# Mixer: convolutions from shifted rows laid out through HBM, output sums in PSUM, pieces spread over slots, light slots filled with zero-weight matmuls

## The chip, the cores and the metric

The kernel runs on one core of one Trainium2 chip, in one launch. A core has five engines with instruction streams of their own: TensorE (PE), VectorE (DVE), ScalarE (ACT), GpSimd (POOL) and SyncE (SP), which here issues the DMAs. They meet only at semaphores. The metric is the time of one execution on the device in microseconds. "PEld" in the profile is PE's loading of weights, which overlaps its matmuls. Everything is in 32-bit floats.

## The reference

Input `x` is 8 sequences of 256 tokens with 128 features. Six blocks are added to it in turn: a network of six small attentions (twice, with a 16-head attention between), a mixture of 8 experts with the best 2 per token, a mixer, and the same experts again.

```python
x = x + 0.5 * ffn(layernorm(x)); x = x + attention(layernorm(x)); x = x + 0.5 * ffn(layernorm(x))
x = x + 0.5 * experts(layernorm(x))
x = x + mixer(layernorm(x))
x = x + 0.5 * experts(layernorm(x))

# mixer, hidden [b, l, 128]; DI = 256 channels, DS = 16 states, DR = 64, K = 4 taps
xz = einsum('bld,ed->bel', hidden, in_proj_w)              # 512 rows: x and z
def branch(xz, ...):                                       # once forward, once on xz[:, :, ::-1]
    x, z = split(xz, 2, axis=1)
    x = silu(causal depthwise convolution(x, conv_w [256, 1, 4]) + bias)
    dt, B, C = x_proj(x)                                   # 64 + 16 + 16 rows
    delta = softplus(dt_proj(dt) + dt_bias)
    h = exp(delta * A) * h + delta * B * x                 # a scan over the tokens, per channel and state
    y = sum over states of h * C + D * x
    return y * silu(z)
# third branch: a 2-D FFT of x, a width-5 convolution over frequencies with 512 x 512 weights, silu,
# an inverse FFT, times max(silu(z)), absolute value, and a layer norm of that: out_f
out = einsum('bdl,od->blo', out_forward + out_backward[:, :, ::-1] + out_f, out_proj_w)
```

The causal convolution of a channel `c` is `sum over k of w[c, k] * x[c, l + k - 3]`: each channel stands alone. The backward branch is the same with the taps counted from the other side.

## The kernel before

The 2048 tokens are 4 chunks of 512 (`NCH` = 4), each of two sequences and of four tiles of 128 tokens. The two networks and the attention come first; the change doesn't touch them. The rest is one function, `experts_and_mixer`. It holds the first experts, the mixer and the second experts, and it writes them as a list of slots.

The mixer's 256 channels are two tiles `t` of 128 partitions, its directions are `r` = 0 and 1. Channel and state are spread over partitions in units: a chunk has 32 units (`t`, `r`, a channel group `i` and a half `jp`), 128 in all. A unit `n` takes these steps:

- `spread`: matmuls with 0/1 weights copy rows of `dl` (delta) and `du` (delta times x) from 32 rows to 128 partitions (line 1197), 32 rows deep. Two go into `pU`, a pair of PSUM banks with two buffers; two go into single banks ("p" banks, three in all), from which ACT makes `dA` = exp(A * delta) (line 1199; four buffers).
- `feed`: DVE multiplies `pU` with `B` (line 1206).
- `scan`: DVE runs the scan (line 1217, two buffers `h`); POOL multiplies `h` with `C` into `hc` (line 1219).
- `sums`: on every second slot, eight matmuls with 0/1 weights add two units' `hc` into the bank of `y`, 32 columns each (line 1236).

Slot `i` holds in this order: scan of unit `i`, feed of unit `i + 1`, the pieces that `at(i, ...)` lists, on odd slots the sums of units `i - 3` and `i - 2`, the pieces listed with `last=True`, then the spread of unit `i + 2` with some units' dA. The order is written out by hand for PE, DVE, ACT and POOL (a manual schedule: each engine takes its instructions in exactly this order). SP has its own queue, and takes its DMAs in the order in which they were written. Slots before 0 are a prologue, where the first experts' 16 tiles are interleaved (`first.step`), and slots after 127 an epilogue with the second experts.

The pieces of a chunk, by their names and lines:

- `normalize` makes the layer norm. `features` transposes it into `xT`, which has three zero columns at either end (line 1059). `gate` makes `sz` from `xT` (line 1069).
- `convolve(ch, t, r)` makes the projection and the convolution in one: four matmuls, one per tap, of 128 x 128 weights and 512 columns, on `xT` at four shifts, summed in a PSUM bank (line 1082). Their weights `inK` are the projection times the tap, multiplied on DVE in `taps` (line 872), where `inK` arrives as a table of 1 MB. ACT copies the result into `u`.
- `ranks`, `rows`, `steps`, `softplus`, `delta` make `B`, `C`, `dl` and `du`. `steps` is two matmuls, 64 rows deep (line 1133). `delta` has a product on POOL (line 1155) and two DMAs that exchange halves of `du` (lines 1158 and 1159).
- `skip` adds `D * u` into the bank of `y` (line 1226); `weigh` multiplies `y` with `sz`.
- The FFT branch: `frequencies`, `pairs` (POOL), `mix` (ten matmuls each, line 1280), `mirror`, `halves` (POOL, line 1306), `over_channels`, `folds` (POOL), `over_tokens` (lines 1312 and 1313 for both), `squares`, `magnitude`, `moments`, `whiten`. It runs up to 32 slots behind the scans of its chunk. Around two slots in a chunk (`bursts`) ACT changes its table for SiLU; no dA is made there, and more of it some slots later.
- `join` adds the FFT branch to `sz` on POOL (line 1416), `output` projects with eight matmuls of 128 columns and copies to `o`, `add` adds `o` to `x` on POOL (line 1437).

In the prologue, chunk 0's convolutions stand in slots -15 to -12. The weights of the FFT branch are folded there too: `fetch` loads 1 MB tables `s_fft` one after the other, `fold_pairs` adds and subtracts them on POOL and DVE (line 921 is a small DMA of each), and `transform` and `conv_weights` multiply them (lines 883 and 934).

Of the kernel before, what the change touches and what calls it, by code (L numbers as in the profile page):

```python
# [17 lines left out]
P = 128  # L18
# [797 lines left out]

def experts_and_mixer(nc, tc, ident, nhalf, x, cols, ins, w, given, store):
# [19 lines left out]
    with ExitStack() as ctx:  # L837
        pool = ctx.enter_context(tc.tile_pool(name="mamba", bufs=1))
        ps = psum(ctx, tc)

# [5 lines left out]
        xT = pool.tile([P, 2, S + 6], F32, name="xT")  # L846
        nc.gpsimd.memset(xT[:, :, 0:3], 0.0)
        nc.gpsimd.memset(xT[:, :, S + 3 :], 0.0)
        xTm = xT[:, :, 3 : S + 3]
# [4 lines left out]

        tiny = pool.tile([P, 1], F32, name="tiny")
# [5 lines left out]
        def at(slot, f, *a, last=False):  # L861
            (after if last else before).setdefault(slot, []).append(lambda: f(*a))
# [5 lines left out]

        def taps(r, t):

            to = w["inK"][:, r, t]
            nc.vector.tensor_tensor(to, to, bcast(w["inT"][:, t * P : (t + 1) * P], K), ALU.mult)
# [172 lines left out]
        def normalize(ch, part):  # L1045
            got = gots[ch]
            h = part % 2
            xh = x[ch][:, 2 * h : 2 * h + 2, :]
            if part < 2:
                got["stats", h] = ln_scales(nc, pool, nhalf, xh, 1e-5)  # L1050
                return
            if h == 0:
                got["xn"] = given["xT"].rearrange("p (t d) -> p t d", t=NT)
            ln_scaled(nc, xh, got["xn"][:, 2 * h : 2 * h + 2, :], got["stats", h])

        def features(ch):
# [5 lines left out]
            nc.scalar.copy(xTm, pt)  # L1062

        def gate(ch, t):
            got = gots[ch]
            if t == 0:
# [3 lines left out]
                pz, w["inT"][:, DI + t * P : DI + (t + 1) * P], xTm, start=True, stop=True  # L1070
            )
            nc.scalar.copy(got["sz"][:, t, :], pz.rearrange("p b l -> p (b l)"))

        def convolve(ch, t, r):
# [5 lines left out]
            for k in range(K):  # L1080
                o = k if r == 0 else 2 * (K - 1) - k
                nc.tensor.matmul(  # L1082
                    pu, w["inK"][:, r, t, k, :], xT[:, :, o : o + S], start=(k == 0), stop=(k == K - 1)
                )
# [20 lines left out]
        def ranks(ch, r):  # L1105

            got = gots[ch]
            if r == 0:
                got["low"] = pool.tile([LOW, 2, CT], F32, tag="low", name="low")
            px = bank([P, CT])[0:LOW, :]  # L1110
            for t in range(2):
                nc.tensor.matmul(  # L1112
                    px, w["xproj"][:, r, t, :], got["u", t][:, r, :], start=(t == 0), stop=(t == 1)
                )
            nc.scalar.copy(got["low"][:, r, :], px)

        def rows(ch, r, k):
# [4 lines left out]
            n = DR + DS * k  # L1122
# [3 lines left out]
        def steps(ch, t, r):  # L1126

            got = gots[ch]
            if r == 0:
                got["dl", t] = pool.tile([P, 2, CT], F32, tag=f"dl{t}", name=f"dl{t}")  # L1130
# [750 lines left out]
```

## Time and profile before

| | us |
|---|---|
| median of three runs (1972.27 to 1981.3) | 1974.96 |
| profiled execution, its own time | 1971.64 |
| its span in the profile | 1969.9 |
| first scan starts | 1352.8 |
| last scan starts | 1896.9 |

Busy in the whole span: PE 1860.1 us (94%), PEld 1143.3, DVE 1503.3 (76%), ACT 1019.3 (52%), POOL 1074.3 (55%). The mean granted clock of TensorE is 0.98 of full speed. These are shares over stages with different limits; the stage that matters here is that of the 128 scans. There a group's row tells, in this order, line, engine, operation, the tile written and those read, shapes, and the count; then the busy time in us, the mean of one in ns, the idle time of the engine just ahead of these instructions, and what ended most of it. A line of waits names the engine and line that waited, the one that ended the wait, the total in us, how often, and the longest. Matmuls overlap each other, so the mean of one is longer than its distance to the next: where a matmul's cost is meant, the distance from one group's start to the next instruction's is taken.

### The profile page before, as it was taken

How to read it: one execution, taken by the hardware profiler on the slowest of the kernel's cores; microseconds unless marked ns; L12 is line 12 of the kernel's file. 1: busy time of each engine (PE TensorE's matmuls, PEld its weight loads, DVE VectorE, ACT ScalarE, POOL GpSimd, SP SyncE). 2: the span in 40 equal slices, each digit the busy share in tenths (PEclk: the TensorE clock that was granted, in tenths of full speed). 3: DMA queues.
4: the chain of work that ended last, by engine and by line, in shares of the span. 5: the costliest groups of instructions: out<-in, count | busy, mean ns of one | idle time of the engine just before them, and what ended most of it. 6: DMA issues, size and time to landing. Idle time of an engine off the chain costs nothing. (4 is left out here: it accounts for less than half of the span.)

```text
span 1969.9 us, 45628 instructions
## 1 busy us (share of the span) xinstructions
PE 1860.1 (94%) x17792; PEld 1143.3 (58%) x17792; DVE 1503.3 (76%) x2573; ACT 1019.3 (52%) x1911; POOL 1074.3 (55%) x1399
## 2 busy tenths in 40 slices
PE   6999999998999999899999999799989999989888
PEld 5777777764565666577777776453344344345345
DVE  5777777787878777577777777647997887997874
ACT  2666666662333222166666666445555654654544
POOL 4333333357666655433333334644878787787864
PEclk9999999998999999899999999999999999999899
DMA  4000000000000000000000000321000010000000
GB/s 151 3 3 3 3 3 3 3 3 1 2 2 2 2 2 2 1 3 3 3 3 4 3 3 3 113 72 26 12 22 22 0 30 15 12 21 12 0 1 22
DMA packets 21242, 29.27 MB, mean 15 GB/s; under 512 B 12506, under 2 KB 13914, under 8 KB 20260
## 3 DMA queue, kind: packets, MB, share of 16 engines
q1 hardware_dynamic: 20740, 26.15, 4.5%
q8 instruction: 142, 2.33, 0.5%
q14 instruction: 72, 0.59, 0.1%
q10 hardware_dynamic: 288, 0.20, 0.0%
HBM read 16.10 MB, written 1.05 MB: 9 GB/s over the span
## 5 line engine op out<-in xcount | busy, mean ns | idle before, releaser
L350 DVE TENSOR_REDUCE negmax<-sc 128x2 f32<-128x512 f32 x768 | 475.0, 677 | 126.7 <-PE sc L342 126.4
L355 ACT ACTIVATE ex<-sc 128x512 f32<-128x512 f32 x768 | 398.0, 603 | 231.9 <-PE sc L342 231.9
L342 PE MATMUL sc<-qk,qk 32*128 32x256 f32 x6144 | 423.1, 397 | 8.0 <-DVE tp L393 2.7
L342 PEld LDWEIGHTS sc<-qk,qk 32*128 32x128 f32 x6144 | 309.8, 187 | 109.7 <-issue 65.5
L1219 POOL TENSOR_TENSOR hc<-h,C 128x1024 f32<-128x1024 f32 x128 | 301.3, 2357 | 112.0 <-DVE h L1217 106.9
L298 POOL TENSOR_SCALAR qk<-qkraw,head_rows,w_bqk 128x256 f32<-128x256 f32 x384 | 207.8, 555 | 203.8 <-ACT qkraw L294 197.8
L1217 DVE TENSOR_TENSOR_SCAN h<-dA,pU 128x1024 f32<-128x1024 f32 x128 | 292.1, 2282 | 13.4 <-POOL hc L1219 0.9
L406 POOL TENSOR_TENSOR cn<-tp,rec 128x256 f32<-128x256 f32 x96 | 59.5, 620 | 287.1 <-DVE rec L404 287.1
L1199 ACT ACTIVATE dA<-p,cols 128x512 f32<-128x512 f32 x256 | 162.1, 684 | 102.8 <-PE p L1197 100.6
L1206 DVE TENSOR_TENSOR pU<-pU,B 128x1024 f32<-128x1024 f32 x128 | 155.7, 1216 | 59.0 <-PE p L1197 51.8
L385 PE MATMUL pc<-ex,va 128*32 128x256 f32 x3072 | 185.7, 382 | 0.3 <-ACT ex L355 0.3
L639 ACT ACTIVATE ex<-sc 128x512 f32<-128x512 f32 x128 | 66.1, 603 | 204.5 <-PE sc L624 204.5
L1197 PE MATMUL pU<-du,s_sel 32*128 32x512 f32 x512 | 146.4, 645 | 19.5 <-DVE h L1217 14.0
L1197 PE MATMUL p<-dl,s_sel 32*128 32x512 f32 x512 | 154.2, 635 | 4.3 <-ACT dA L1199 4.2
L624 PE MATMUL sc<-rot,rot 32*128 32x256 f32 x2048 | 135.2, 388 | 0.3 <-POOL rot L607 0.3
L385 PEld LDWEIGHTS pc<-ex,va 128*32 128x32 f32 x3072 | 90.0, 109 | 78.1 <-ACT ex L355 28.0
L642 POOL TENSOR_TENSOR both<-ex 128x512 f32<-128x512 f32 x64 | 80.0, 1271 | 71.7 <-ACT ex L639 71.7
L624 PEld LDWEIGHTS sc<-rot,rot 32*128 32x128 f32 x2048 | 97.9, 184 | 35.1 <-issue 22.6
L634 DVE TENSOR_REDUCE anegmax<-sc 128x2 f32<-128x512 f32 x128 | 79.4, 683 | 22.1 <-PE sc L624 22.1
L1197 PEld LDWEIGHTS pU<-du,s_sel 32*128 32x128 f32 x512 | 40.3, 185 | 89.6 <-issue 65.2
L393 DVE STREAM_TRANSPOSE tp<-pc 128x512 f32<-128x512 f32 x96 | 68.6, 715 | 28.0 <-PE pc L385 28.0
L1010 POOL TENSOR_TENSOR sg_hT<-sg_hT,hid 128x512 f32<-128x512 f32 x32 | 40.5, 1267 | 65.9 <-ACT sg_hT L1009 65.9
(293 smaller groups left out, 3098.7 us busy)
## 6 DMA issues: line engine op xcount, KB each, us to landing
qk<-turned SPq DMA_DIRECT2D x768, 1.0 KB
s_fft<-s_fft SPq DMA_DIRECT2D x5, 1024.0 KB
du<-ab SPq DMA_DIRECT2D x16, 256.0 KB
B<-low SPq DMA_DIRECT2D x64, 32.0 KB
C<-low SPq DMA_DIRECT2D x64, 32.0 KB
x<-x SPq DMA_DIRECT2D x4, 256.0 KB
s_inK<-s_inK SPq DMA_DIRECT2D x1, 1024.0 KB
out<-x SPq DMA_DIRECT2D x4, 256.0 KB
```

What stands on the lines that cost most here:

```text
L298: nc.gpsimd.tensor_scalar(t[:, g, :], raw[:, i, :], w["mask"][:, g : g + 1], w["bqk"][:, c, i, g : g + 1], ALU.mult, ALU.add,)
L342: nc.tensor.matmul(sc[:, t, :], lhs[:, t * P : (t + 1) * P], rhs, start=True, stop=True)
L350: nc.vector.tensor_reduce(sh[:, :, 4 * g + j], sc, AX.X, ALU.max, negate=True)
L355: nc.scalar.activation(ex, sc, AF.Exp, scale=FD**-0.5)
L385: nc.tensor.matmul(st["pc"][32 * j : 32 * j + 32, g, :], st[2][:, kt, 2 * j + g, :], st["ex", g, j][:, kt, :], start=(kt == 0), stop=(kt = ...
L624: nc.tensor.matmul(sc[j][:, t, :], lhs[r, part, t * P : (t + 1) * P] if part < 2 else sel[r, :], rhs[r, part, :] if part < 2 else st["nm"] ...
L642: nc.gpsimd.tensor_tensor(both, ex[:, :, 0], ex[:, :, 1], ALU.add)
L1197: nc.tensor.matmul(dst, w["sel"][rs, i, :], src[rs, :], start=True, stop=True)
L1199: nc.scalar.activation(dA, pA, AF.Exp, scale=rate)
L1206: nc.vector.tensor_tensor(dB, dB, bcast(gots[ch]["B", r], 2), ALU.mult)
L1217: nc.vector.tensor_tensor_scan(hf, af, bf, 0.0, ALU.mult, ALU.add)
L1219: nc.gpsimd.tensor_tensor(hc, h, bcast(gots[ch]["C", r], 2), ALU.mult)
```

## The change

- **Convolution.** A new piece `inputs(ch, t)` does the projection alone (one matmul), copies it to SBUF, writes its rows to HBM in four DMAs, and reads them back in four more, into `shifted`: there partition `32 k + c` holds row `c` of each group of 32 channels, shifted by `k` tokens, so that the four taps of a channel lie on four partitions. `convolve` becomes four matmuls, one for each group of 32 channels, with a 128 x 32 matrix of taps (`s_taps`, 256 KB), each into 32 partitions of the PSUM bank. `taps` and the 1 MB table `s_inK` go; `xT` loses its zero columns, and shares a buffer with `mag`, the copied rows share one with `sq`.
- **Steps.** `low` of direction 1 puts `dt` on partitions 64 to 127, so that the two directions' matmuls of `steps` use different rows of the array; they stand together, each into a bank of its own.
- **Output.** `join` and `add` go. `output(ch, h)` does a half of the tiles: PSUM sums the gated term, the FFT term and `x` itself (times the identity), 10 matmuls of 128 columns, and ACT copies the sum into `x`.
- **Spreads.** The order of a spread's matmuls goes by the rows that they use; where two units' dA are made in a slot, it is listed in `wide`, and the bursts move so that the dA keep their parity.
- **Slots.** Pieces move: `inputs` at slots 2 and 10 of the count that starts a chunk ahead of its scans, `convolve` at 6, 8, 13 and 14 (before at 2, 6, 8, 10), `steps`, `delta`, `mix`, `halves` and what follows them some slots later, `pairs` in four single steps. Chunk 0 has `inputs` last in slots -15 and -13, `convolve` two at a time in -13 and -11.
- **Filler.** `keep_busy`: in slots 0 to 127, where PE's work by a table (`work`) is under `BUSY` = 1.9 us, as many matmuls with zero weights, 128 x 128 on 256 columns, as fill it. They add zero to the bank of `y`, or go to an empty one.

```diff
-        def taps(r, t):
-
-            to = w["inK"][:, r, t]
-            nc.vector.tensor_tensor(to, to, bcast(w["inT"][:, t * P : (t + 1) * P], K), ALU.mult)
...
+        def inputs(ch, t):
+
+            px = bank([P, 2, S])
+            xT = gots[ch]["xT"]
+            nc.tensor.matmul(px, w["inT"][:, t * P : (t + 1) * P], xT, start=True, stop=True)
+            xs = pool.tile([P, 2, S], F32, tag="sq", name="xs", bufs=2)
+            nc.scalar.copy(xs, px)
+            there = hbm.tile([32, 4, 2, S], F32, tag="xs", name="xs_rows")
+            for g in range(4):
+                nc.sync.dma_start(out=there[:, g], in_=xs[32 * g : 32 * g + 32])
+            for k in range(K):
+                nc.sync.dma_start(
+                    out=shifted[32 * k : 32 * k + 32, :, :, K - 1 - k : K - 1 - k + S],
+                    in_=there,
+                )
...
-            for k in range(K):
-                o = k if r == 0 else 2 * (K - 1) - k
+            for g in range(4):
                 nc.tensor.matmul(
-                    pu, w["inK"][:, r, t, k, :], xT[:, :, o : o + S], start=(k == 0), stop=(k == K - 1)
+                    pu[32 * g : 32 * g + 32],
+                    w["taps"][:, r, t, g, :],
+                    shifted[:, g, :, 3 * r : 3 * r + S],
+                    start=True,
+                    stop=True,
                 )
...
+            pds = [bank([P, CT]) for _ in range(2)]
+            for r, pd in enumerate(pds):
+                rs = slice(DR * r, DR * r + DR)
+                nc.tensor.matmul(
+                    pd,
+                    w["dtT"][rs, t * P : (t + 1) * P],
+                    got["low"][rs, r, :],
+                    start=True,
+                    stop=True,
+                )
...
+        def keep_busy(k):
+
+            y = live.get("y")
+            to = bank([P, S]) if k and y is None else y
+            for _ in range(k):
+                nc.tensor.matmul(
+                    to[:, 0:S], zeros, w["G"][:, 0, 0, :], start=y is None, stop=y is None
+                )
...
-        def join(ch):
-            got = gots[ch]
-            nc.gpsimd.tensor_tensor(
-                got["sz"], got["sz"], got["mag"].rearrange("p t b l -> p t (b l)"), ALU.add
-            )
...
+            terms = (got["sz"], got["mag"].rearrange("p t b l -> p t (b l)"))
+            po = bank([P, 2, D])
+            for i in range(2):
+                t = 2 * h + i
+                for v, y in enumerate(terms):
+                    for d in range(2):
+                        nc.tensor.matmul(
+                            po[:, i, :],
+                            y[:, d, t * P : (t + 1) * P],
+                            w["outT"][:, d, :],
+                            start=(v == d == 0),
+                            stop=False,
+                        )
+                nc.tensor.matmul(po[:, i, :], ident, x[ch][:, t, :], start=False, stop=True)
+            nc.scalar.copy(x[ch][:, 2 * h : 2 * h + 2, :], po)
-        def add(ch):
-            nc.gpsimd.tensor_tensor(x[ch], x[ch], gots[ch]["o"], ALU.add)
...
-        for i in range(4):
-            at(-15 + i, convolve, 0, 1 - i // 2, i % 2)
-        at(-11, gate, 0, 0)
-        at(-10, gate, 0, 1)
+        for t in (1, 0):
+            at(-13 - 2 * t, inputs, 0, t, last=True)
+            at(-14, gate, 0, 1 - t)
+            at(-11 - 2 * t, convolve, 0, t, 0)
+            at(-11 - 2 * t, convolve, 0, t, 1)
...
-                at(o + 2, convolve, ch, 1, 0)
-                at(o + 6, convolve, ch, 1, 1)
-                at(o + 8, convolve, ch, 0, 0)
-                at(o + 10, convolve, ch, 0, 1)
...
+                at(o + 2, inputs, ch, 1)
+                at(o + 10, inputs, ch, 0)
+                at(o + 3, gate, ch, 0, last=True)
+                at(o + 4, gate, ch, 1, last=True)
+                at(o + 6, convolve, ch, 1, 0)
+                at(o + 8, convolve, ch, 1, 1)
+                at(o + 13, convolve, ch, 0, 0)
+                at(o + 14, convolve, ch, 0, 1)
...
-            mixes = (4, 6, 8, 9, 11, 12, 14, 15) if final else (11, 13, 18, 20, 22, 23, 24, 25)
+            mixes = (4, 6, 7, 8, 12, 13, 14, 15) if final else (8, 12, 18, 20, 22, 24, 26, 28)
...
-            k = o + (17 if final else 27)
+            k = o + (17 if final else 30)
             bursts.add(k)
             if not final:
-                bursts.add(o + 12)
+                bursts.add(o + 15)
+                wide |= {o + 22, o + 23, o + 34, o + 35}
...
-                    more = next(((0, 0, 1, 2, 1, 1, 2)[i - b] for b in bursts if 0 <= i - b < 7), 1)
+                    more = 0 if i in bursts or i - 1 in bursts else 2 if i in wide else 1
+                busy = 0.43 * (1 + more) + 0.85 * (i % 2)
+                busy += sum(work.get(f, 0) for f, _ in before.get(i, []) + after.get(i, []))
+                if 0 <= i < N:
+                    keep_busy(max(0, math.ceil((BUSY - busy) / 0.43)))
```

## The prediction

> **What bounds the kernel now.** I read the page's slices first, then cut the span by stage (windows), then asked in the stage that changes who waits for whom (the waits and the groups), and last followed one stretch piece by piece (the chain). The change touches only the mixer: its prologue before the first scan at 1352.8 us, its 128 scan slots, and its epilogue after 1896.9 us. The windows below are the prologue, the four chunks of 32 scans, and the epilogue; columns are window, length, busy time of each engine (instructions), clock of PE, DMA share, GB/s.
>
> ```profile
> 1245.00:1352.80 107.80, 95.23 (x408) 55.73 (x411) 54.27 (x154) 57.22 (x96) 49.50 (x67) 0.98 0.29 96
> 1352.80:1481.60 128.80, 120.09 (x540) 46.98 (x540) 119.37 (x82) 72.69 (x114) 95.22 (x67) 0.97 0.06 14
> 1481.60:1619.00 137.40, 129.84 (x618) 57.00 (x616) 119.27 (x87) 79.39 (x125) 111.03 (x86) 1.00 0.07 16
> 1619.00:1756.20 137.20, 129.77 (x617) 57.00 (x616) 118.08 (x78) 79.37 (x125) 108.11 (x78) 1.00 0.07 16
> 1756.20:1896.90 140.70, 125.44 (x609) 62.40 (x609) 116.34 (x102) 65.11 (x107) 114.74 (x85) 0.94 0.03 7
> 1896.90:1969.90 73.00, 59.99 (x322) 39.68 (x320) 38.46 (x126) 36.50 (x63) 34.64 (x39) 0.97 0.04 15
> ```
>
> In the middle chunks DVE works 118 to 119 of 137 us, PE shows 130, POOL 108 to 111. A slot needs the scan (2.28) and the feed (1.21) on DVE, 3.54 us start to start when nothing is late; 32 of them are 113, and DVE's other work (weigh, delta, largest, statistics) makes about 123 us a chunk. So about 14 us of a middle chunk are lost. To whom, in the scan stage (total us, times, longest):
>
> ```profile
> POOL hc L1219 <- DVE h L1217: 105.7, 66, 6.7
> DVE pU L1206 <- PE p L1197: 51.8, 48, 5.2
> PE pU L1197 <- DVE h L1217: 14.0, 13, 2.5
> ```
>
> DVE, at the feed, waits for PE's spread; PE waits back for the scan only 14 us in 544. POOL waits for DVE, so it has room on average. Whether PE is late by work or by a wait is told by one stretch, 1619 to 1681, where twelve of these waits (12.1 us) lie; the chain there:
>
> ```profile
> by line: PE pU L1197 23.7%; PE p L1082 23.5%; PE p L1312 12.8%; PE p L1313 10.4%; PE py L1236 9.6%; PE p L1197 6.5%; PE p L1280 4.0%; POOL sp L1306 3.8%; PE py L1226 3.4%; PE p L1069 3.1%; ACT dA L1199 1.1%; PE p L1059 0.7%; issue 0.1%
> ...
> 1634.18 3.63 PE p L1082 x8
> 1637.82 0.62 PE pU L1197
> ...
> 1669.17 3.64 PE p L1082 x8
> ```
>
> It is PE's own work, and the convolution (L1082) is nearly a quarter of it: 3.64 us in a slot of 3.54. The second loss is the clock:
>
> ```profile
> 1778.40:1781.80 3.40, 1.48 (x7) 0.79 (x6) 3.27 (x3) 0.76 (x2) 3.40 (x3) 1.00 0.00 0
> 1781.80:1785.20 3.40, 3.40 (x8) 2.64 (x9) 0.93 (x1) 0.60 (x1) 3.40 (x3) 0.50 0.02 5
> ```
>
> After 3.4 us in which PE was busy for 1.48, the next 3.4 us ran at half clock, and the slot that started at 1780.4 took 8.86 us. The loop has five such stretches, 24 us in sum (also at 1385.9, 1457.6, 1839.8, 1867.2).
>
> **The change, part by part.** Durations by rows of this execution:
>
> ```profile
> L1236 PE MATMUL py<-hc,s_ysel 128*32 128x512 f32 x496 | 66.9, 612 | 0.0
> L1082 PE MATMUL p<-xT,s_inK 128*128 128x512 f32 x96 | 46.2, 625 | 0.3 <-DVE w_conv L950 0.3
> L1069 PE MATMUL p<-xT,s_inT 128*128 128x512 f32 x12 | 6.0, 621 | 0.0
> L1416 POOL TENSOR_TENSOR sz<-sz,mag 128x1024 f32<-128x1024 f32 x3 | 7.1, 2355 | 0.0
> L1437 POOL TENSOR_TENSOR x<-x,o 128x512 f32<-128x512 f32 x3 | 3.8, 1265 | 0.0
> ```
>
> (a) Convolution. Four matmuls into 32 columns each replace four full ones. The sums (L1236) have that very shape and leave in 1.00 us from start to next, the old convolution in 3.64: -2.64 x 4 = -10.6 us of PE a chunk. The new inputs matmul has the shape of L1069, .96, twice: +1.9. Two steps' matmuls run side by side in row groups: -1.8 a chunk.
>
> (b) Output. Twenty matmuls of 128 columns replace eight, 4.6 against 2.0 us: +2.6 of PE. The join and the add on POOL go, 2.36 + 1.27 = -3.6 us. The copy into x moves to ACT (65 to 79 of 137 busy, so covered).
>
> (c) Spreads. A pair on distinct row groups costs 1.05, one on the same groups 1.92, a triple 2.4 to 2.7. Lining up the dA parity saves about 3.5 us of PE a chunk.
>
> (d) Filler. About ten zero matmuls of .43 a chunk, in light slots only: +4.5 of PE where PE waits for DVE anyway. That waiting is its cover; if the cover is gone, up to 4.5 a chunk is lost.
>
> Net in heavy slots: -10.6 + 1.9 - 1.8 + 2.6 - 3.5 = -11 us a chunk. What of it reaches DVE is read from the idle time before the feeds (L1206), slot by slot. Scans 64 to 76 show 1.99, .85, 2.61, 1.40, .20, .34, 1.06, .34, 1.05, .34, 1.06, .89: 12.1 us; 49 to 53 and 58 add 3.6, so 15.7 in a middle chunk. In the new order I carried PE's lateness from slot to slot (its work less 3.54; a spread waits for the scan two before it). One wait stays: the first over-channels product, in the second slot of the next chunk, stands behind POOL's second half (2.37, begun after late hc), 3.9 us; then follow a gate, inputs and a wide spread, and the feeds lose 2.0, .8, 1.35 and .4, 4.5 us. So 15.7 becomes 4.5, -11 a middle chunk. The same count over the old order finds only 9.9 of the 15.7 and gives -6.5, so I take -8, twice. Chunk 0 loses little in either order (-1); chunk 3 keeps its bunched order of mixes and products: 0. Sum -17; ends -12 (only the four convolution slots, 2.61 + 1.06 + 1.05 + 1.06, twice) and -24.
>
> (e) Clock. Filled slots have 1.9 of 3.54 us, .54; the windows before drops show .25 to .40 (one .63), windows of .42 and above mostly none. The five stretches cost the loop 10 to 14 us by their slots; chunk 3's pass to other waits in part. I take -8, ends 0 and -14. The Trainium skill, TensorE: Matmul & The Clock Gate, Part 1, speaks against this: half clock comes after at least one idle window of about 3.4 us, and a window with 1.48 us of work isn't idle. By that rule filler would hold nothing, and this term would be 0 or +2; the row above shows a drop after such a window, so I go by the row.
>
> (f) The trip through HBM. After inputs' copy (.59) come four issues and four reads on SP:
>
> ```profile
> L1159 SPq DMA_DIRECT2D du<-ab x8: 596/596/597, 1341.4 to 1772.8; - x8
> ...
> SPq L1876 <- DMA out<-x: 1.8, 1, 1.8
> ```
>
> An issue is .60, and the last output store (256 KB to HBM) was seen done 1.8 us after its issue. Four issues, landing, four issues, landing: 8 x .6 + 2 x 1.8 = 8.4 us, less .6 to 1 where a first issue overlaps; 7.4 to 8.4. In the loop the convolution stands four slots (t=1, 14.2 us) or three (t=0, 10.6) behind; .96 + .59 + 8.4 = 10 just fits, so 0, ends 0 and +2 at each of three places. SP issues this behind du's copies, which wait for POOL's product; those are two slots earlier.
>
> In the prologue the distance is one slot, about 4 us. Convolve (0,1) and then (0,0) hold PE, in order, with first experts' steps queued behind. PE idle there: 8 less what stands between, about 5.5 and 7, plus about 1.7 each at half clock afterwards (a 5.5 us gap ending at 1250.0 was followed by matmuls of .85 instead of .43). +16. Against it, PE is lighter: 13.8 of convolution becomes 5.7, -8. Taps (3.0 on DVE) and a 1 MB load are gone, -1. Net +7, ends -3 (the fold of the conv weights on POOL and DVE is late anyway and covers it) and +14 (the reads also queue behind fold's copies in SP's order).
>
> (g) Epilogue: output moves in two halves, join and add go; ends -2 and +2, 0.
>
> Sum: -17 - 8 + 0 + 7 + 0 = -18. The profiled execution took 1971.6 (span 1969.9), 3.3 under the median 1975.0. 1971.6 - 18 = 1953.6; on the median's scale 1957. A change under 0.5%, 9.9 us, can't be told from none.
>
> **The rivals.** *The trip is too long* (slower). If it takes 15 us, not 8, then t=0 convolutions wait 6 us in each of three chunks; the spread runs 2.5 us ahead of its feed, so 3.5 reach DVE, +10.5; each gap drops the clock, which gives back 5; the prologue pays twice 7 more, +14. -18 + 30 = +12: 1987. It turns slower than before at about 13 us. For it: eight issues in one queue, two dependent landings. Against: the 1.8 us landing. The skill's page DMA: Bandwidth & Descriptors, Anatomy of one DMA, gives about 2 us a DMA and warns of a surprisingly long delay to HBM; two such would make 8.8 by my sum. *POOL becomes the bound* (same). Its work falls only from 114 to 110 of 123 us, and pairs, halves and folds still come in bursts; if every PE gap becomes a wait at h or hc, (a) to (d) yield -5: 1969. *The filler doesn't hold the clock*: (e) is 0: 1965. *PE is out of the way altogether*, the prologue's stalls being covered: -24 - 14 + 0 = -38: 1937.
>
> **How the numbers follow.** Forecast .45 (own range 1946 to 1969), trip .17, POOL .13, filler .10, all of it .15. Faster by over 0.5% (under 1965): .45 x .88 + .10 x .5 + .13 x .1 + .15 = .61. Slower (over 1985): .17 x .75 + .03 from the unknown ends of (f) and POOL = .16, raised to .20, since so many moved pieces can collide in ways that this count lacks (ACT's banks, SP). Same .19. The range leaves out the far end of the trip and of the full gain: 1932 to 1992.
>
> **What would show it.** Right: convolve groups of 1.0 us; the feed's wait for PE in the loop at 25 or less; no half clock between 1353 and 1880; PE gaps of 5 to 7 us at the two prologue convolutions; middle chunks of 125 to 131. Wrong: PE waits for a DMA at convolve in the loop; POOL's wait for h shrinks while scans wait for hc; half-clock stretches with filler in them; a prologue longer by over 14.

## The result, and the profile after

The changed kernel is slower: 2004.18 us median (1997.34 to 2007.86) against 1977.91 for the kernel before beside it, a ratio of 1.0143 with a 95% interval of 1.0116 to 1.017. The profiled execution took 2001.43 us, its span is 1999.6. The forecast was 1957 with a range of 1932 to 1992.

Cut by stage, the windows of the kernel after, for the prologue from 1245 us to the first scan, the 127 slots from the first scan to the last, and the rest (columns: window, length, busy time of PE, PEld, DVE, ACT, POOL with instructions, clock of PE, DMA share, GB/s):

```profile
1245.00:1378.90 133.90, 95.56 (x412) 54.85 (x411) 51.58 (x150) 58.71 (x97) 48.73 (x65) 0.85 0.32 91
1378.90:1918.60 539.70, 499.51 (x2559) 225.09 (x2560) 473.68 (x347) 299.55 (x479) 419.72 (x299) 0.97 0.13 28
1918.60:1999.60 81.00, 67.44 (x348) 45.23 (x346) 39.66 (x126) 37.45 (x64) 31.15 (x37) 0.90 0.04 14
```

The same three stages before:

```profile
1245.00:1352.80 107.80, 95.23 (x408) 55.73 (x411) 54.27 (x154) 57.22 (x96) 49.50 (x67) 0.98 0.29 96
1352.80:1896.90 544.10, 505.14 (x2379) 223.37 (x2380) 473.06 (x347) 296.55 (x470) 429.10 (x313) 0.98 0.06 13
1896.90:1969.90 73.00, 59.99 (x322) 39.68 (x320) 38.46 (x126) 36.50 (x63) 34.64 (x39) 0.97 0.04 15
```

So the 29.7 us of span are: prologue +26.1, scan loop -4.4, epilogue +8.0. The forecast had +7, -25 and 0. Since executions differ by a few us before the mixer begins, the table below counts the prologue from the mixer's first product on POOL, `w_D`, to the first scan: 107.3 us before, 132.0 after, +24.7. The clock fell outside of the loop too: half clock rose from 3.4 to 41.0 us in the prologue, and from 3.4 to 13.7 ahead of the last matmuls of the epilogue.

The waits of the prologue show what fills it (engine, line, what ended the wait; total us, times, longest):

```profile
PE p L1119 <- DMA shifted<-xs_rows: 23.4, 2, 13.0
```

PE waits twice at a convolution for the rows that come back from HBM. The timeline of the second wait, first SP's queue, then PE (start, us, engine, line, operation):

```profile
1322.18 0.24 SPq L927 DMA_DIRECT2D pairs<-s_fft  x1
1322.47 1.71 SPq L1105 DMA_DIRECT2D xs_rows<-xs  x4
1324.29 0.38 SPq L910 DMA_DIRECT2D s_fft<-s_fft  x1
1325.55 2.50 SPq L1107 DMA_DIRECT2D shifted<-xs_rows  x4
...
1318.10 1.02 PE L1100 MATMUL p<-xT,s_inT 128*128 128x512 f32 x2
...
1335.13 2.79 PE L1119 MATMUL p<-shifted,s_taps 128*32 128x512 f32 x12 [12.96 <-DMA shifted<-xs_rows]
```

The copy of the rows ended at 1319.89. SP stood behind a fold's DMA until 1322.18. The four reads were asked for until 1328.05, their packets ran from 1328.27, behind a 1 MB load, to 1334.20, and PE began at 1335.13.

In the loop the feeds still wait for PE:

```profile
DVE pU L1258 <- PE p L1249: 43.5, 34, 4.2
PE pU L1249 <- DVE h L1269: 14.7, 15, 2.0
```

43.5 us against 51.8 before. By chunks of 32 scans the loop went from 128.8, 137.4, 137.3 and 140.6 (31 scans) to 122.7, 140.9, 136.2 and 139.8; DVE's idle time ahead of feeds and scans, counted where it is over 0.14 us, went from 6.0, 14.8, 15.7 and 17.2 to 0, 17.3, 13.9 and 18.6. In chunk 1 it stands for the most part in four places: slots 36 to 39 lose 5.2 us, 44 and 45 lose 5.0, 49 and 50 lose 2.3, and 56 to 60 lose 3.5. Only chunk 0, whose slots hold no piece of an earlier chunk, became even. Half clock remains: 30.7 us of the loop in six stretches (before 23.9 in five). One of them, with what stood before it:

```profile
1557.20:1560.60 3.40, 1.43 (x11) 0.54 (x4) 2.36 (x2) 1.27 (x3) 3.40 (x3) 1.00 0.79 143
1560.60:1564.00 3.40, 3.40 (x9) 2.23 (x7) 1.16 (x1) 0.49 (x1) 3.40 (x3) 0.50 0.00 0
```

PE's work in a middle chunk did not fall. From each matmul to the next, waits left out, chunk 2 holds 129.8 us before and 130.2 after:

| us of PE in chunk 2 | before | after |
|---|---|---|
| convolve, inputs | 14.5 | 3.9 + 1.9 |
| spread | 45.8 | 46.2 |
| output | 2.0 | 4.9 |
| steps | 3.9 | 3.0 |
| filler | 0 | 5.1 |

In these sums a matmul at half clock counts its longer time, and a spread that waits for a bank in its middle only its matmuls.

### The profile page after: what moved, and what is told of

Its sections match the earlier page's. It is cut to its first block, busy times and chain, and to the rows that moved or that the text cites. A ratio compares the mean times of both kernels' runs of the same rounds, so it can differ in the third digit from the quotient of the medians.

```text
span 1999.6 us, 46130 instructions
## 1 busy us (share of the span) xinstructions
PE 1862.3 (93%) x18002; PEld 1151.5 (58%) x18002; DVE 1503.0 (75%) x2569; ACT 1025.1 (51%) x1923; POOL 1060.1 (53%) x1380
## 5 line engine op out<-in xcount | busy, mean ns | idle before, releaser
L1258 DVE TENSOR_TENSOR pU<-pU,B 128x1024 f32<-128x1024 f32 x128 | 155.5, 1215 | 51.6 <-PE p L1249 43.5
L1249 PE MATMUL p<-dl,s_sel 32*128 32x512 f32 x512 | 164.6, 660 | 0.0
L1249 PE MATMUL pU<-du,s_sel 32*128 32x512 f32 x512 | 149.3, 656 | 15.7 <-DVE h L1269 14.7
L1012 DVE TENSOR_TENSOR hid<-ph,gate 128x1024 f32<-128x1024 f32 x32 | 39.0, 1220 | 79.9 <-PE ph L1007 75.0
```

The costliest lines, as they stand in the source:

```text
L1249: nc.tensor.matmul(dst, w["sel"][rs, i, :], src[rs, :], start=True, stop=True)
L1258: nc.vector.tensor_tensor(dB, dB, bcast(gots[ch]["B", r], 2), ALU.mult)
```

## The experiments

The stages of every run, in us; the ratio is to the kernel before, run beside it, with its 95% interval. "Half clock" is the sum of the stretches in the loop, where the granted clock was 0.5.

| run | prologue | loop | epilogue | half clock | ratio |
|---|---|---|---|---|---|
| before | 107.3 | 544.1 | 73.0 | 23.9 | 1 |
| after | 132.0 | 539.7 | 81.0 | 30.7 | 1.0143 (1.0116 to 1.017) |
| e1, trips apart | 123.8 | 538.1 | 81.1 | 30.7 | 1.0099 (1.0084 to 1.0114) |
| e2, no filler | 131.8 | 551.2 | 79.9 | 71.7 | 1.0189 (1.0174 to 1.0204) |
| e4, xs in its own place | 134.9 | 550.4 | 80.7 | 44.4 | 1.0176 (1.0143 to 1.021) |
| e5, output as before | 131.6 | 536.0 | 74.9 | 37.5 | 1.0101 (1.0081 to 1.0121) |
| e6, no first trips | 106.1 | 542.9 | 80.6 | 37.5 | 1.0033 (1.0021 to 1.0046) |
| e8, heavy convolution | 141.5 | 564.4 | 81.0 | 37.5 | 1.0303 (1.0277 to 1.0329) |
| e10, no wide spreads | 128.9 | 527.8 | 78.1 | 30.7 | 1.0053 (1.0035 to 1.0071) |
| e11, more filler | 131.6 | 543.4 | 77.9 | 10.2 | 1.0132 (1.0107 to 1.0157) |
| b1, before with filler | 109.4 | 544.7 | 73.0 | 17.1 | 1.0032 (1.0013 to 1.005) |
| b2, before, filler by room | 107.3 | 544.0 | 73.0 | 17.1 | 0.9998 (0.9987 to 1.0009) |
| v1, first chunk and output old | 120.2 | 536.8 | 75.6 | 37.5 | 1.0014 (1.0001 to 1.0027) |
| v2, v1 with pieces moved | 116.9 | 546.7 | 75.4 | 68.3 | 1.0082 (1.0065 to 1.0098) |
| v3, v2 with filler by room | 120.1 | 547.2 | 74.6 | 78.5 | 1.0095 (1.0071 to 1.0119) |
| v4, v1 with taps later | 109.6 | 533.4 | 75.3 | 23.9 | 0.9984 (0.9968 to 1.0) |
| v5, v4 without wide spreads | 109.7 | 527.5 | 74.9 | 44.4 | 0.9933 (0.991 to 0.9957) |

The stages are those of one execution each, the profiled one. How far they carry shows in loops that hold the same instructions: those of after, e1 and e6 took 539.7, 538.1 and 542.9, those of e5, v1 and v4 536.0, 536.8 and 533.4. So a few us between two loops show nothing by themselves; the ratios, from 4 to 12 executions each, decide.

### The prologue's trips

The first edit moves chunk 0's pieces only:

```diff
-            at(-13 - 2 * t, inputs, 0, t, last=True)
+            at(-13 - 3 * t, inputs, 0, t, last=True)
...
-            at(-11 - 2 * t, convolve, 0, t, 0)
-            at(-11 - 2 * t, convolve, 0, t, 1)
-        at(-9, ranks, 0, 0)
+            at(-9 - 4 * t, convolve, 0, t, 0)
+            at(-9 - 4 * t, convolve, 0, t, 1)
+        at(-8, ranks, 0, 0)
```

> The changed kernel with chunk 0's pieces moved alone: inputs of t=1 last in slot -16 and its convolutions in -13, inputs of t=0 last in -13 and its convolutions in -9, ranks with the others in -8. Theory (the prologue's two trips through HBM are most of the loss): in the changed kernel PE waited 10.4 and 13.0 us for shifted; here 2 or 3 slots of about 4 us stand between, so the waits fall to under 5 us in sum and the time by 15 to 19 us, to about 1987, no different from before by over 1%. Rival (the prologue is held by the fold of the FFT weights, and PE's idle time there costs nothing): the waits go and the time falls by under 5 us, since the first scan moves by under 5.

Measured: 8.2 us less prologue, ratio 1.0099 against 1.0143. The waits of the prologue in this run:

```profile
PE p L1119 <- DMA shifted<-xs_rows: 15.7, 2, 8.2
```

Between the two expectations: the waits cost time, but two or three slots don't cover a trip there. From the end of a copy to the last packet it took 16.5 us for t = 1 and 16.3 for t = 0 in this run. In the first, SP stood behind a fold's fetch, which waited 3.2 us for POOL, before it could ask for the reads. In the second it stood behind a fold's small DMA for 2.6 us before the writes, and the reads' packets took 7.7 us (5.3 in the loop) while loads of 1 MB were under way. That `shifted` has one buffer held up neither: the first convolution began at 1306.99, the second trip's reads were asked for at 1322.17, as soon as its writes had landed.

The next takes the trips away:

```diff
         def inputs(ch, t):
...
+            if ch == 0:
+                return
```

> The changed kernel without the two trips of chunk 0: its inputs stop after the matmul, and its convolutions read a shifted that is zero everywhere (chunk 0's mixer output is left wrong by that; all else is computed). This takes away what PE waits for, 23.4 us. Theory (the prologue's two trips are 19 to 26 us of the loss, the spread trips of the first experiment having still waited 15.7): scan 0 starts 20 to 26 us earlier, at 1353 to 1359, and the run takes 1974 to 1984. Rival (the first scan is held by something behind, the weights' fold or DVE's delta): under 12 us earlier.

Measured: 106.1 us of prologue, 25.9 less. This is the whole of the prologue's loss, and it says two things. The trips cost 26 us where their two waits are 23.4; and a prologue with the light convolutions but without any trip is only 1.2 us shorter than the old one, so next to nothing of the lighter PE is seen there. Why is open. On the chain that ended last the kernel before has the four convolutions with 13.9 us and the products of `conv_weights` with 1.9; e6 has the products with 14.5 in their place, and 17.1 us of half clock in its prologue where the kernel before has 3.4. Yet the run is still 0.33% above the kernel before: the loop and the epilogue give nothing back in sum.

### The output

```diff
-            at(k + rest[4], output, ch, 0)
-            at(k + rest[5], output, ch, 1)
+            at(k + rest[4], join, ch)
+            at(k + rest[5], output, ch)
+            at(k + rest[6], add, ch)
```

> The changed kernel with the output part undone: join and add on POOL again, output once per chunk with eight matmuls. Theory (twenty matmuls instead of eight cost PE 2.7 us where PE is the bound, which is the epilogue and the slots where a half stands beside a mix): the epilogue is 3 to 4 us shorter, the loop 1 to 4 us shorter. Rival (POOL's 3.6 us a chunk come back as waits for hc): the loop is 3 to 8 us longer and the sum slower.

Measured: the epilogue is 6.1 us shorter, the loop 3.7; ratio 1.0101. The theory stands in the epilogue, and more so than expected: there PE's matmuls are 54.9 of the 81.0 us on the chain that ended last in the changed kernel, and 34.6 of 74.9 in this run. Half clock ahead of its last matmuls fell from 13.7 us in three stretches to 6.8 in two, which is worth half of that by my estimate, and so the output's extra matmuls, 2.9 us, are about half of the 6.1. The 3.7 of the loop are within what equal loops differ by; between the means of the two sets of three above it is 4.8. POOL's work, 3.6 us a chunk, came back without a wait that shows.

### The filler and the clock

```diff
-BUSY = 1.9
+BUSY = 0.0
```

> The changed kernel with BUSY = 0, so without the zero-weight matmuls (they add nothing to any sum). Theory (filler neither holds the clock nor delays the feeds): time within 4 us of the changed kernel's, half-clock stretches in the scan loop 30 to 45 us in sum against its 31. First rival (filler makes PE late, which is why the loop gained 4 us and not 25): 8 to 15 us faster. Second rival (filler does hold the clock, as forecast): 5 to 12 us slower, with two or more further half-clock stretches.

Measured: the loop is 11.5 us longer, with 71.7 us at half clock in place of 30.7. The second rival is right: filler holds the clock, and my theory before this run, that it hardly matters, was wrong. The larger finding stands beside it: without filler the loop of the changed kernel has three times the half clock of the kernel before (23.9). So the change leaves more stretches with little work, and the filler buys back no more than that. Whether the lighter convolutions or the moved slots make them, no run separates; against the convolutions alone speaks the run with heavy ones below, whose loop has 37.5 us at half clock with the same filler.

```diff
-BUSY = 1.9
+BUSY = 2.6
```

> The changed kernel with BUSY = 2.6 in place of 1.9, some ten more zero-weight matmuls a chunk. Theory (the half clock that is left comes from waits inside slots that are full by the table, which more filler in light slots doesn't reach): half-clock stretches in the loop stay at 20 to 40 us, the loop within 4 us. Rival (1.9 us were too few): the stretches fall under 15 us and the loop is 5 to 9 us shorter.

The loop's windows with more filler, and with none:

```profile
1380.00:1923.40 543.40, 526.53 (x2722) 251.58 (x2723) 475.54 (x347) 298.30 (x478) 419.81 (x299) 0.99 0.13 28
```

```profile
1378.60:1929.80 551.20, 494.56 (x2463) 213.99 (x2464) 473.88 (x346) 299.19 (x479) 419.57 (x299) 0.93 0.12 27
```

More filler, some 83 further matmuls in the loop, nearly ends half clock: 10.2 us, clock 0.99. Over all executions the mean clock of the whole kernel is 0.975 to 0.977, against 0.964 to 0.970 with 1.9 us and 0.957 to 0.961 without filler. Yet the time doesn't fall: this loop is 3.7 us longer than with 1.9, and the ratios, 1.0132 and 1.0143, can't be told apart. So of the two expectations neither holds as a whole: 1.9 were too few for the clock, and the clock that came back was worth no time. PE is busy for 27 us more (526.5 against 499.5); where that makes the loop late isn't shown, for the feeds wait as long for PE as before (43.8 and 43.5 us). At 31 us of half clock the rest of the clock's price is about what the filler that ends it costs.

The filler alone, in the kernel before, by the same rule and by the room of each slot:

```diff
+                if 0 <= i < N:
+                    keep_busy(max(0, math.ceil((BUSY - busy) / 0.43)))
```

> The kernel before with the filler alone, by the same rule (1.9 us a slot, the old pieces' work in the table). Theory (filler holds the clock where slots are light, as its removal showed, 11.6 us in the loop of the changed kernel): the five half-clock stretches, 24 us, fall to 10 or less and the time falls by 5 to 12 us against before. Rival (the stretches come from waits that filler by slots doesn't fill): within 3 us of before.

```diff
+        long = {delta: 2.1, weigh: 0.68, largest: 1.5, moments: 1.2, conv_weights: 1.37}
...
+                room = 3.54 + sum(long.get(f, 0) * (f is not delta or v[2] == 0) for f, v in was)
+                was = before.get(i, []) + after.get(i, [])
+                busy = 1.13 * busy
+                k = math.ceil((BUSY / 3.54 * room - busy - late) / 0.45)
...
+                late = max(0, late + busy + 0.45 * k - room) if i >= 0 else 0
```

> The kernel before with filler measured by the room of a slot: DVE's long pieces of the slot before (delta 2.1 us, weigh, largest, moments) lengthen it, and PE's backlog, carried from slot to slot, is taken off. Theory (drops come behind delta, where a slot lasts 5.8 us and not 3.54, and filler in late slots costs feeds): 2 to 5 us faster than with the plain rule, 8 to 16 faster than before. Rival: no difference to the plain rule beyond 2 us.

Measured: half clock in the loop falls from 23.9 to 17.1 in both, and the time does not: 1.0032 and 0.9998. The expectation of 5 to 12 us was wrong, the rival right. By room is 0.3% better than by the plain rule, which is about the size expected of it, on a gain that isn't there; it also puts in less, some 16 filler matmuls in the loop where the plain rule puts 47.

### The weight of the convolution

```diff
-            for g in range(4):
+            for g in 4 * (0, 1, 2, 3):
```

> The changed kernel with each convolution's four matmuls issued four times over (each overwrites the one before, so the sums stay the same): the convolution weighs 4.0 us on PE again, as before the change it did with 3.64, and all else is new. My forecast's step (a): the loop pays most of 12 us a middle chunk, so it is 15 to 25 us longer. Rival theory (a lighter PE loses to half clock what it wins, and the slots of the convolutions are not those that are late): the loop is 0 to 8 us longer, with the half-clock stretches in it falling from 31 us.

Measured: the loop is 24.7 us longer and the feeds wait for PE 68.4 us in place of 43.5:

```profile
POOL hc L1271 <- DVE h L1269: 122.3, 69, 6.7
ACT dA L1251 <- PE p L1249: 108.7, 108, 3.2
DVE pU L1258 <- PE p L1249: 68.4, 50, 4.2
```

So step (a) of the forecast is right in size. A convolution takes 3.57 us in this run and 1.00 in the changed kernel; 2.57 us on each of twelve are 31 us of PE, and the loop pays 25 of them, some 3 of which may be the 6.8 us more at half clock. At the old 3.64 it would be about 25 too (24.7 x 2.64 / 2.57, an estimate). The convolution won on PE what was forecast, and other parts of the change lost some 21 of it again in the loop.

### The squares' buffers

```diff
-            xs = pool.tile([P, 2, S], F32, tag="sq", name="xs", bufs=2)
+            xs = pool.tile([P, 2, CT], F32, tag="ab", name="xs")[:, 0, :]
+            xs = xs.rearrange("p (b l) -> p b l", b=2)
```

> The changed kernel with the copied rows xs in the buffer of ab, which is free at those slots, not in one of the two buffers of sq. Theory (over-tokens' squares wait for a buffer that xs holds: ACT waited 16.0 us for POOL's mag in five places, and the feeds of scans 44, 45 and 76 lost 7.2 us behind it): that wait falls to under 5 us, the loop is 5 to 8 us shorter. Rival (POOL is late by then in any case, and PE would wait for its folds instead): under 2 us.

Measured: ACT's wait for `mag` fell from 16.0 to 3.1 us, as the theory had it, and nothing was won. The idle time at the feeds in slots 44 to 47 fell from 5.0 to 3.2 us, that in 76 to 79 rose from 2.2 to 3.9, and ACT's wait for PE at the same squares rose from 14.5 to 21.3. The loop is 10.7 us longer, with 44.4 us at half clock, in an execution that is the slowest of four (2001.86 to 2016.68); that the edit makes the kernel slower isn't shown, since the intervals of the ratios overlap. So the buffer was not what made those feeds late. That POOL is late there in any case, as the rival says, and why the clock fell more often aren't shown.

### The wide spreads

A change of ACT's table costs two slots without a unit's dA, and two wide slots that catch up. In the changed kernel a wide spread takes 2.99 us from its start to the next matmul (two in each middle chunk 3.5 to 4.4, where the clock fell), an aligned one 1.07: four matmuls run at once, but the two of the second unit come one after the other, the last of them behind ACT, which has to free one of three banks. The kernel before has four wide spreads in a middle chunk too, of 2.96 to 3.81 us. The edit leaves no slot without a unit:

```diff
-                    more = 0 if i in bursts or i - 1 in bursts else 2 if i in wide else 1
+                    more = 1
```

> The changed kernel with one unit's dA in every slot: none left out at the changes of ACT's table, and so no wide spreads. Theory (the four wide spreads of a chunk, 2.99 us each where an aligned one is 1.07, stand in slots that are full already, and the feeds of 36, 37, 56, 68, 69, 88, 100 and 101 lose 16 us behind them): the loop is 8 to 14 us shorter. Rival (ACT is late at the table changes, and scans wait for dA there; or PE, lighter still, falls to half clock more): the loop changes by under 4 us, with idle time ahead of scans from ACT or more half clock than 31 us.

The windows and the waits of its loop:

```profile
1378.50:1906.30 527.80, 479.54 (x2549) 216.56 (x2549) 473.44 (x346) 298.65 (x479) 419.81 (x299) 0.97 0.13 29
```

```profile
DVE pU L1258 <- PE p L1249: 31.1, 32, 3.1
```

Measured: the loop is 11.9 us shorter, at the same 30.7 us of half clock, and the feeds wait 12.4 us less. The theory holds. The feeds' losses in slots 36, 37, 68, 69, 100 and 101, 13.1 us in the changed kernel, became 1.3, and those in 56 to 60 and 88 to 92, 7 us, went below what is counted (0.25 a slot). Against that, 32, 33, 64 and 65, beside the change of the table, lose 10.3 us in place of 1.5. The prologue and the epilogue, which the edit hardly touches, are about 3 us shorter each in this execution, so the ratio holds more than the loop's gain.

### Towards a version that beats both

v1 undoes what the runs above showed to cost: the output, and the trips of chunk 0, whose convolutions use the full weights again (they lie in the room that `shifted` takes from slot -5 on).

```diff
+        inK = pool.tile([P, 2, 2, K, P], F32, tag="shifted", name="inK")
+        nc.sync.dma_start(out=inK, in_=ins["s_inK"])
...
+            for k in range(K if ch == 0 else 0):
...
+            for g in range(4 if ch else 0):
```

> The changed kernel with two parts undone: the output as before (eight matmuls, join and add on POOL), and chunk 0's convolutions as before (full weights made from the 1 MB table in the room that shifted takes later; shifted is laid out from chunk 1 on). Theory (the loss is the prologue's trips, 26 us, and the output, 11 us, and the loop's convolutions are a gain): scan 0 at 1349 to 1354, the loop 535 to 538 us, the epilogue 75, so 1961 to 1970, 0 to 12 us faster than before. Rival (the trips' 26 us were partly due to the load and the fold behind them, which come back with the 1 MB table): scan 0 at 1360 or later, slower than before.

Measured: a prologue of 120.2 us, ratio 1.0014. The rival was half right, by a wait of another kind. The 1 MB table is now asked for behind all other weights, and DVE waits for it in slot -23:

```profile
DVE inK L866 <- DMA inK<-s_inK: 9.4, 1, 9.4
```

v2 moved four pieces of v1 out of full slots:

```diff
-                at(k + ((4, 5, 6, 7) if final else (3, 4, 6, 8))[i], over_channels, ch, i // 2, i % 2, last=True)
+                at(k + ((4, 5, 6, 7) if final else (4, 5, 7, 9))[i], over_channels, ch, i // 2, i % 2, last=True)
-                wide |= {o + 22, o + 23, o + 34, o + 35}
+                wide |= {o + 22, o + 23, o + 32, o + 33}
-            mixes = (4, 6, 7, 8, 12, 13, 14, 15) if final else (8, 12, 18, 20, 22, 24, 26, 28)
+            mixes = (4, 6, 7, 8, 12, 13, 14, 15) if final else (8, 12, 18, 20, 24, 25, 26, 28)
-                at(o, features, ch, last=True)
+                at(o + 1, features, ch)
```

> The version before in this list, with four pieces moved: over-channels one slot later (4, 5, 7, 9 in place of 3, 4, 6, 8), the second wide pair from slots 34 and 35 to 32 and 33, the third pair of mixes to 24 and 25, features one slot later. Theory (the feeds' remaining loss stands where heavy pieces share a slot: 34 to 37 lost 6.2 us a chunk, 56 to 60 lost 3.5, 65 lost 1.5): 5 to 12 us off the loop. Rival (the lateness only moves to other slots and the clock falls elsewhere): within 3 us.

Measured: the loop is 9.9 us longer, with 68.3 us at half clock. The rival is right. A slot behind delta that lost its mix became so light that the clock fell for 17 us on end in three of the chunks; the feeds in slots 24 to 26, which had lost nothing, lost 7.2 us there. The mean clock of all six executions is 0.961 to 0.969, v1's 0.969 to 0.976.

v3 adds to v2 the filler by the room of a slot, with the same lines as b2.

> The same with filler measured by the room of a slot (DVE's long pieces of the slot before lengthen it, PE's backlog is taken off). Theory (half clock comes where slots are stretched): 2 to 6 us faster than with the plain rule. Rival (drops come from waits in the middle of heavy slots): within 2 us.

Measured: no better, 1.0095 against 1.0082, with 78.5 us at half clock. Filler by room, some 29 matmuls in the loop where v2 has 54, doesn't repair it.

v4 is v1 with the taps' products in slots -19 to -16:

```diff
-            at(-23 + i, taps, i // 2, i % 2)
+            at(-19 + i, taps, i % 2, 1 - i // 2)
```

> The version with chunk 0's convolutions and the output as before, with the four products of the taps on DVE in slots -19 to -16 in place of -23 to -20: there DVE waited 9.4 us for the 1 MB table, which is now asked for behind all other weights, and the experts' steps and PE behind it. Theory (that wait is what held its scan 0 at 1369): scan 0 at 1352 to 1358, the loop as it was (535 to 538), 8 to 14 us faster than it, 4 to 12 faster than the kernel before. Rival (the fold's fetches, now behind that table in the queue, hold the prologue): under 5 us.

Measured: 109.6 us of prologue, 1969.05 us, ratio 0.9984, which can't be told from the kernel before.

> Both edits together: chunk 0's convolutions and the output as before, taps in slots -19 to -16, one unit's dA in every slot. By the theories of the two: scan 0 at 1352 to 1358, a loop of 522 to 530, so 1950 to 1962, 10 to 22 us faster than the kernel before. By the rivals: within 5 us of it.

Measured: 1958.95 us, ratio 0.9933 (0.991 to 0.9957). It beats both kernels: 13.7 us faster than the one before. Its prologue, loop and epilogue:

```profile
1250.00:1359.60 109.60, 96.25 (x408) 56.01 (x411) 54.11 (x155) 57.37 (x96) 47.91 (x65) 0.97 0.29 98
1359.60:1887.10 527.50, 476.10 (x2481) 211.07 (x2480) 475.16 (x347) 298.12 (x476) 430.35 (x305) 0.96 0.13 29
1887.10:1962.00 74.90, 62.56 (x324) 40.58 (x322) 38.49 (x126) 36.90 (x63) 34.66 (x39) 0.94 0.04 15
```

It keeps from the change the light convolutions of chunks 1 to 3, the steps side by side, the moved slots and the filler. What each of them is worth in it isn't taken apart.

## Why the prediction was wrong, point by point

The forecast missed the prologue by 17.7 us, the two terms of the loop (-17 and -8) by 20.6 together, and the epilogue by 8.0.

**The trip through HBM, step (f), is the single term that missed most.** The forecast took 7.4 to 8.4 us, from issues of .60 and a landing of 1.8. In the loop it took 9.6 to 10.5 from the end of the copy to the last packet (for instance 1513.99 to 1524.29), and PE began .9 us after the last packet where it stood waiting. The landing that I took was that of a single store of 256 KB. Each of the four reads also moves 256 KB, 1 MB together, in 1024 packets of 1 KB; they took about 82 ns each and 5.3 us on the queues. In the loop that just fits: once, in chunk 0, PE stood 1.4 us at a convolution that began .95 us after the last packet (the profile puts this wait down to ACT), and no feed was late for it. In the prologue it took 14.3 both times. SP is held by the fold's DMAs, which the forecast named and left to the far end of its range (2.0 and 2.6 us before the writes), and writes or reads run behind a load of 1 MB, which it didn't name: the second trip's reads began 2.7 us after SP asked for them, 1.4 in the loop. Waits of 10.4 and 13.0 came of 5.5 and 7. And of the -8 set against them for PE's lighter work, the run without trips shows -1.2; why no more isn't shown. +7 became +24.7.

**Step (a), the convolution, was right** in its mechanism and size: 3.9 us a chunk for four, and about 25 us of the loop by the heavy run.

**What of it reaches DVE was wrong.** I counted -11 us of PE a chunk for heavy slots and let 4.5 us of lateness remain, at one place. The measured lateness is 17.3 and 13.9 in the middle chunks, at four places for the most part in the first of them. By chunks I had -1, -8, -8 and 0; measured were -6.1, +3.5, -1.1 and -0.8, so what the loop gained, it gained in chunk 0, of which I expected 1 us. The feeds' wait for PE, which was to fall to 25 us or less, is 43.5. Of the terms: the spreads' -3.5 did not come. Waits left out, they take 45.8 us of PE in either middle chunk before, and 45.6 and 46.2 after. A wide one, priced at 2.4 to 2.7, is 2.96 to 3.81 in the old trace already, and 2.99 or, where the clock fell, 3.5 to 4.4 in the new one; they stood beside over-channels, gates and mixes, and taking them away was worth 11.9. Steps came to 1.06 for the pair of t = 0, as forecast, but to 1.92 for that of t = 1, whose second matmul waits for a bank that ACT has to free; so -1.8 was -0.9. The output cost 2.9 for 2.6, and 3.7 of the loop. The 21 us that the loop lost against the convolution's 25 are not taken apart further, and their cause stays open: the old kernel has as many wide spreads, so 11.9 is what they cost, not their difference to the old order; and half clock, filler and lateness change together in each run.

**Step (e), the clock, had the right mechanism and the wrong balance.** That filler holds the clock, as the row of 1778 led me to take, is borne out in the changed kernel: 71.7 us at half clock without it, 30.7 with 1.9 us a slot, 10.2 with 2.6. The rule of the Trainium skill (TensorE: Matmul & The Clock Gate, Part 1) puts half clock after at least one idle window of about 3.4 us. The window at 1557.2 shows again that such a window can hold work, 1.43 us of it before half clock. What failed is "I take -8": I set the filler against the old kernel's five stretches and didn't ask how many a lighter and reordered PE would add. In the old kernel itself the same filler took half clock only from 23.9 to 17.1 us and won no time. The margin was misread too. The windows ahead of the five old drops hold 0.99 to 1.58 of 3.40 us of PE's busy time in four cases (.29 to .46, not .25 to .40) and 2.49 in one; and in the changed kernel the window from 1574.3 held 1.82 of 3.40, the .54 of a filled slot, and half clock followed. Nor is filler free under PE's waiting, as part (d) had it: at 2.6 the clock was nearly whole and the time the same.

**Step (g), the epilogue at 0,** named no cover for the 2.6 us that part (b) put on PE. There PE's matmuls are 54.9 of 81.0 us on the chain that ended last (32.8 of 73.0 before), with 10.2 us more at half clock than before, and it was +8.0, of which 6.1 go with the output.

**Of the rivals,** the trip that is too long came nearest. Its price for the prologue, 14 on top of 7, is about what was measured; its price for the loop was not paid. The skill's figure of about 2 us (DMA: Bandwidth & Descriptors, Anatomy of one DMA) is the fixed part of a DMA that GpSimd issues, and the page sets beside it a part that grows with the bytes. My 8.8 for the trip took the fixed part alone; the reads' packets measured 5.3 us. POOL did not become the bound: POOL's hc waited for DVE 105.7 us in the loop before and 103.9 after.

## What to carry to other kernels

Price a round trip through memory by all of its packets and by everything that is ahead of it in the issuing queue; a trip that is hidden in the steady state can stand bare in the prologue. When an engine under a clock gate is made lighter or its work is moved, ask where its quiet stretches will be: part of the gain can go to a lower clock, and filler that brings the clock back takes PE's time for it. Judge a piece by the slot it stands in, not by its chunk's sum: four wide spreads in full slots cost half of what the lighter convolutions won.

## What the runs showed of the hardware

Three "p" banks set the price of matmuls that could run side by side. Two of 64 rows in different row groups took 1.06 us as a pair when two banks were free, and 1.92 when the second waited for one that ACT had to free; four of 32 rows took 1.07, and a wide spread, which needs four p banks, 2.99. Packets of 1 KB read from HBM took 79 to 84 ns each in the changed kernel, those of 2 KB written to it 126 to 133 in its loop. And four moves that left PE's work the same, but for some four filler matmuls more, nearly doubled the loop's half clock (37.5 to 68.3 us): the drops follow the order of the work within a few microseconds, not its sum.
